# Three edits of a planner's ranks and margins in the FFN of a perceiver layer

## The chip, the core and the metric

The kernel runs on one NeuronCore of a Trainium2 chip. The metric is the device time of one launch in microseconds. A profile of one execution is shown beside it; its times count from the first instruction of the span.

## What is computed

The reference is one layer with three residual blocks on 16 x 64 rows of 1024 (1024 rows in all, in float32):

```python
x = x + cross_attention(layernorm(x), ctx, ctx, mask)      # 32 query heads, 8 kv heads, 1601 keys
s = silu(layernorm(x) @ w_gate.T)                          # 2752 columns
s[the K = 1376 smallest |s| of each row] = 0               # top_k(-abs(s), k)
x = x + (s * (layernorm(x) @ w_up.T)) @ w_down.T
logits = layernorm(x) @ router_w.T + router_b              # 8 experts, 2 chosen per row
x = x + sum over chosen e of gate[e] * (layernorm(x) @ A[e].T) @ Bm[e].T * 0.5
```

The change lies in the second and third blocks, which the kernel runs together as its FFN phase.

## The kernel before

The 1024 rows are eight tiles of 128 rows. The first half of the span (to about 840 us) is attention. The FFN phase takes the tiles in four pairs: pair n is tiles 2n and 2n + 1. For every pair there are three products with large weights, named in the code g (gate), u (up) and d (down): g0 to g3, u0 to u3, d0 to d3. Each is a Strassen-like scheme: instead of eight quarter products it has seven, each with a sum of quarters of the rows and a sum of quarters of the weights. The sums of the weights are made during attention and lie in DRAM (`ts`).

The stages of one pair are:

- Normalising (`normed`, from `measured`): ACT computes a mean and a sum of squares, POOL makes the inverse root and a shift, ACT scales the row tile. The rows are first loaded again from DRAM (`xs`) into the tile `s`.
- `quad_turned` transposes four blocks on PE (`pt_f` in the trace) and copies them out of PSUM on ACT. `gate` adds the four sums of quarters in `hS`, on DVE for the first pair and on POOL for the others.
- `widen` runs the units of g and u: one unit is one of seven products on one of four chunks of columns, eight matmul rows of the trace (`pg_g`, `pg_u`), about 2.3 us. DVE and ACT sum the products; ACT applies silu to g, POOL multiplies u in.
- `drop_small` is the choice of the zeroed elements. It is a search over 31 bits for a threshold per row; each step is a compare on DVE (`junk`) for the first tile of the pair, a sign on ACT (`sign`) for the second, and a short settling on DVE (`cand`). Scans follow on DVE (`rank`), and POOL multiplies the zeros into `s`.
- `turned` transposes `s` (`ptd` on PE, copies on ACT), and `down` runs d: seven products (in the order 1, 5, 7, 6, 2, 3, 4), each in four parts (`pd`). The row sums that it needs are made on POOL in parts (`S`, and sums in place in `s`). DVE and POOL add the products to the residual `xd`.
- `experts` runs once per tile, after its two sums of d: it transposes x (`pt_m`, copied to `xT`), multiplies by the router and the A matrices (`pl`), chooses, transposes (`ph`) and multiplies by Bm (`py`); DVE writes the result, and SP stores it.

The order of instructions on PE, DVE, ACT and POOL is not written by hand. Every piece above is a task with an engine, a cost in microseconds, the tasks it depends on, a rank, and the buffers it takes and frees. `Plan.run` walks through planned time. Whenever an engine is free, it starts the task of lowest rank (and of earliest creation among equals) whose dependencies have ended and whose buffers are free. A task with a margin also waits until each dependency has ended for that long. The order in which tasks are started is the order in which they are emitted, and each of these four engines then runs its own list strictly in that order.

The ranks that matter here are these. Copies and sums are at 0. The transposes of the experts are at 0 or -1. The last signs and the scans of a choice are at 2, the compares and signs of its search at 3. Normalising for pairs 1 to 3, and transposing and summing for their gates, are at 5. The large products have ranks 10, 20, ... by their place in one list, and the transposes and sums on POOL of a d follow the rank of that d (one lower, or the same):

```python
order = ["g0", "u0", "g1", "g2", "d0", "u1", "g3", "d1", "u2", "d2", "u3", "d3"]
rank = {name: 10 + 10 * j for j, name in enumerate(order)}
```

Three groups of buffers bind the stages. Five PSUM banks (`pg`) serve all large products. Two PSUM banks (`px`) serve all transposes and the experts. One hold named `opening` is taken by the first unit of every chunk of g and u and by the first part of every d, and is given back by product 7 of the chunk or by the first part of product 6 of the d. Two tiles of sums (`hS`) exist, so gate 3 can be transposed only when u1 has read the tile of pair 1. Tiles 6 and 7 also reuse the `s` tiles of tiles 0 and 1, so their rows are loaded after the results of those tiles are stored, and their normalising has a margin of 30 us after that start.

Weights come through a ring of six tiles, loaded by DMAs on SP: one of 688 KB per unit of g or u, and one of 768 or 512 KB per part of a d.

Of the kernel before, what the change touches and what calls it, by code (L numbers as in the profile page):

```python
# [21 lines left out]
B, S, D = 16, 64, 1024  # L22
T, C = 1601, 256
HD = 32
NT = B * S // P
# [29 lines left out]
def tile_perceiver_layer(  # L55
# [306 lines left out]
    def finish_tile(i, h, home=ps_t, tag="pt"):  # L362


        if h == 0:
            att[i] = xnp.tile([P, 2, 4, 4, HD], F32, tag="xn", name=f"att{i}")
        rows = att[i][:, h]
        pt = home.tile([P, 4, P], F32, tag=tag, name=f"pto{i}_{h}")
        for r in range(4):
            pe.transpose(  # L370
                pt[:, r, :], oT[i][:, h, r].rearrange("p b s -> p (b s)"), ident
            )

        def add():
            pool.tensor_tensor(
                rows, rows, rs_tok[i][:, h].unsqueeze(3).to_broadcast([P, 4, 4, HD]),
                ALU.mult,
            )
            xv = x[i].rearrange("p (h g r d) -> p h r g d", h=2, g=4, r=4)
            pool.tensor_tensor(xv[:, h], xv[:, h], rows, ALU.add)  # L380

        return (rows, pt.rearrange("p r (g d) -> p r g d", g=4)), add
# [34 lines left out]
    first, first_xn = (xnp, otp), {}  # L417
    for n in range(ng):
        i, m = n // 8 + 1, n % 8
# [10 lines left out]
        for d in range(2):  # L430
            add = None
# [6 lines left out]
            if n > 8 and 3 <= 2 * m + d <= 4:  # L438
                copy, add = finish_tile(i - 2, 1 - d)
# [89 lines left out]
    def px_tile(shape, name):  # L529
        return ps_x.tile(shape, F32, tag="px", name=name)  # L530

    plan = Plan({"pg": 5, "px": 2, "u": 2, "v": 3, "hS": 2, "opening": 1, "S1": 1})
    add = plan.add
    s, hS, held_h, hs, a, marked = {}, {}, {}, {}, {}, {0: [], 1: []}
# [16 lines left out]
        nc.sync.dma_start(w, home[q, :, c0:c1])  # L551
        return w

    def quad_turned(src, dst, rank, name, after, takes=None):

        box, px = {}, plan.hold("px")

        def turn():
            pt = px_tile([P, 4, P], f"pt_{name}")
            for j in range(4):  # L560
                pe.transpose(pt[:, j, :], src()[:, j * P : (j + 1) * P], ident)
            box["pt"] = pt

        def copy():
            act.copy(dst(), box["pt"])

        t = add("PE", 0.55, turn, after, rank, takes=(px, takes))
        return add("ACT", 0.55, copy, [t], 0, frees=px)

    def measured(rows, junk, rank, name, after, margin=0.0, on_dve=0):  # L570
# [44 lines left out]
    def normed(rows, xn, rank, name, after, margin=0.0):  # L615

        box, t = measured(rows, xn, rank, name, after, margin)

        def shift():
            box["shift"] = small.tile([P, 1], F32, tag="shift", name=f"shift_{name}")  # L620
            pool.tensor_tensor(box["shift"], box["minus"], box["rstd"], ALU.mult)

        def scale():
            act.activation(xn(), rows(), AF.Identity, bias=box["shift"], scale=box["rstd"])

        t = add("POOL", 0.3, shift, [t], rank)
        return add("ACT", 1.1, scale, [t], rank)
# [89 lines left out]
    def gate(pair, n, rank, after):  # L717
        i1, i2 = pair
        engine, name, cost = (dve, "DVE", 0.62) if n == 0 else (pool, "POOL", 1.25)
        turned, ahead = [], 5 if n else rank  # L720
        held_h[n] = plan.hold("hS")

        def quarters(q):
            if n not in hS:
                hS[n] = hsp.tile([P, 7, NH // 2, P], F32, tag="hS", name=f"hS{n}")
            return hS[n][:, q]

        for i in pair:

            def start(i=i):  # L730
                s[i] = sp[i % 6 > 1].tile([P, NIB * P], F32, tag="s", name=f"s{i}")
                pool.memset(s[i][:, I:], 0.0)
                if i not in first_xn:
                    nc.sync.dma_start(s[i][:, D : 2 * D], xs[i])

            t = add("POOL", 0.1, start, after(i), rank)
            if i not in first_xn:
                t = normed(
                    lambda i=i: s[i][:, D : 2 * D], lambda i=i: s[i][:, :D], ahead,
                    f"f{i}", [t], 30.0,  # L740
                )
            for half, q in enumerate((A11, A12) if i == i1 else (A21, A22)):
                turned.append(
                    quad_turned(
                        lambda i=i, half=half: first_xn.get(i, s[i])[
                            :, half * HC : (half + 1) * HC
                        ],
                        lambda q=q: quarters(q), ahead, f"f{i}_{half}", [t] + turned[:1],
                        None if turned else held_h[n],
                    )  # L750
                )

        def summed(dst, q0, q1, op):
            return lambda: engine.tensor_tensor(
                *(hS[n][:, q].rearrange("p k t -> p (k t)") for q in (dst, q0, q1)), op
            )

        hs[n] = turned
        t11, t12, t21, t22 = turned
        t1 = add(name, cost, summed(S1, A21, A22, ALU.add), [t21, t22], ahead)  # L760
        t2 = add(name, cost, summed(S2, S1, A11, ALU.subtract), [t1, t11], ahead)
        t3 = add(name, cost, summed(S3, A11, A21, ALU.subtract), [t1, t11], ahead)
        t4 = add(name, cost, summed(S4, A12, S2, ALU.subtract), [t2, t12], ahead)
        ready = {1: t11, 2: t12, 3: t4, 4: t22, 5: t1, 6: t2, 7: t3}
        return widen(0, n, pair, rank, f"g{n}", lambda p: [ready[p]] + (p == 6) * [t1, t3], None)
# [317 lines left out]
    def experts(i, after):  # L1083
# [15 lines left out]
        def h3T():  # L1099
            if "xT" not in box:  # L1100
                xT = sump.tile([P, NB * P], F32, tag="S1", name=f"xT{i}")
                box["xT"] = xT[:, :D].rearrange("p (c t) -> p c t", c=NH)
            return box["xT"]
# [71 lines left out]
        def copy():  # L1175
# [4 lines left out]
        norm, t = measured(  # L1180
            lambda: x[i], lambda: s[i][:, :D], 1, f"m{i}", after,
            on_dve=(1 + i % 2) * (i >= NT - 2),
        )
        copies, pl, ph = [], plan.hold(kind), plan.hold(kind)
        xT, first = plan.hold("S1"), i % 2
        for g in (first, 1 - first):
            copies.append(
                quad_turned(
                    lambda g=g: x[i][:, g * HC : (g + 1) * HC],
                    lambda g=g: h3T()[:, 4 * g : 4 * g + 4, :], urgent, f"m{i}_{g}",  # L1190
                    after[g : g + 1] + copies + ([logits_of[i - 1]] if i % 2 else []),
                    xT if g == first else None,
                )
            )
        tl = add("PE", 2.1, logits, copies, urgent, takes=pl, frees=xT)
# [12 lines left out]
        t = add("DVE", 1.2, choose, [tb], 1)  # L1208
        t = add("DVE", 0.5, weigh, [te, t], 1)
        add("DVE", 0.6, normaliser, [t], 1)  # L1210
        t = add("PE", 0.2, turn, [t], 0, takes=ph)
        t = add("ACT", 0.3, copy, [t], 0, frees=ph)
# [19 lines left out]
        return done  # L1232

    pairs = [(i, i + 1) for i in range(0, NT, 2)]
    order = ["g0", "u0", "g1", "g2", "d0", "u1", "g3", "d1", "u2", "d2", "u3", "d3"]
    rank = {name: 10 + 10 * j for j, name in enumerate(order)}
    gated = [gate(pairs[0], 0, rank["g0"], lambda i: [])]

    t = add("PE", 2.9, lambda: groups[-1].values(0, NTC), [], rank["g0"] - 5)
    t = add("ACT", 0.3, lambda: groups[-1].keep(), [t], 0)  # L1240
# [8 lines left out]

    over = add("PE", 1.1, end, [t] + hs[0], rank["g0"] - 5)  # L1250
    gated += [gate(pairs[n], n, rank[f"g{n}"], lambda i: [over]) for n in (1, 2)]

    box_ra, held_ra = {}, plan.hold("px")
# [10 lines left out]
    t = add("DVE", 1.3, sum_blocks, [over], rank["g1"], margin=30.0)  # L1264
    t = add("PE", 0.25, sum_rows, [t], rank["g0"], takes=held_ra)
# [4 lines left out]
    for n, pair in enumerate(pairs):  # L1270
        kept, t = drop_small(
            pair, n, gated[n], chosen,
            lambda t: widen(1, n, pair, rank[f"u{n}"], f"u{n}", lambda p: t, t),
        )
# [12 lines left out]
class Plan:  # L1287
# [20 lines left out]
    def add(self, engine, cost, emit, deps, rank, takes=None, frees=None, margin=0.0):  # L1308
        holds, frees = (
            [hold for hold in (h if isinstance(h, tuple) else (h,)) if hold]  # L1310
            for h in (takes, frees)
        )
        task = self.Task(engine, cost, emit, deps, rank, holds, margin)
        for hold in frees:
            hold.freed_by = task
        self.tasks.append(task)
        return task
# [98 lines left out]
```

## Time and profile before

| | |
|---|---|
| median of 3 runs | 1720.96 us (1720.15 to 1721.5) |
| the profiled execution | 1721.3 us |
| its span, first to last instruction | 1719.5 us |
| mean granted TensorE clock | 0.995 |
| busy PE, DVE, ACT, POOL | 1694.0, 1413.0, 1259.6, 557.2 us |
| attention, to about | 840 us |
| pd rows of d0, about | 1127 to 1196 us |
| pg_u rows of u1, about | 1112 to 1258 us |
| pd rows of d1, about | 1265 to 1413 us |
| pg_g rows of g3, about | 1308 to 1378 us |
| pd rows of d2 | 1501 to 1571 us |
| pd rows of d3 | 1633 to 1706 us |

PE is the TensorE's matmuls and PEld its weight loads, DVE is VectorE, ACT ScalarE, POOL GpSimd and SP the engine that issues most DMAs. A row of the timeline has its start, its duration in microseconds (of one instruction, or of several merged), and the operation with the tiles it writes and reads; a number in brackets at its end is the time its engine stood idle before it and the instruction that ended the wait. PEclk is the share of its full clock that TensorE was granted.

### The profile page before, as it was taken

The numbers are of one execution on the slowest core, as the hardware profiler recorded it, in microseconds if no ns is written. First come the engines' busy times: TensorE is split into PE (matmuls) and PEld (weight loads), VectorE is DVE, ScalarE is ACT, GpSimd is POOL, SyncE is SP. The second block draws the span as 40 slices with busy tenths as digits, with TensorE's granted clock in tenths as the row PEclk, the third lists the DMA queues.
The fourth block names the chain that finished last, engine by engine and source line by source line (L and its number), as shares of the span: only waits on it lengthen the run. The fifth ranks groups of instructions, "written<-read, shape, count | busy, mean of one in ns | idle before, by whom it ended". The sixth has DMA issues, their size and how long they took to land. (4 is left out here: it accounts for less than half of the span.)

```text
span 1719.5 us, 38732 instructions
## 1 busy us (share of the span) xinstructions
PE 1694.0 (99%) x15102; PEld 1152.2 (67%) x15102; DVE 1413.0 (82%) x3655; ACT 1259.6 (73%) x1780; POOL 557.2 (32%) x584
## 2 busy tenths in 40 slices
PE   8999999999999999999999999999989999999999
PEld 6777777777777777777766666655645646645644
DVE  7888888888888888888627999999999989999703
ACT  5999999999999999999544676577657782778010
POOL 2045454454444454110120211222282013331631
PEclk9999999999999999999999999999999999999999
DMA  8246456555556646121499999988969978888984
GB/s 248 74 122 207 148 194 210 188 166 195 170 185 206 204 159 208 57 75 58 182 349 324 308 292 304 302 267 291 324 202 292 309 251 301 283 294 270 316 265 143
DMA packets 132327, 384.56 MB, mean 224 GB/s; under 512 B 9489, under 2 KB 61233, under 8 KB 132145
## 3 DMA queue, kind: packets, MB, share of 16 engines
q1 hardware_dynamic: 113280, 312.83, 55.5%
q0 software_dynamic: 18432, 68.16, 12.1%
q8 instruction: 120, 1.97, 0.5%
q10 hardware_dynamic: 432, 1.09, 0.2%
q14 instruction: 63, 0.51, 0.1%
HBM read 339.58 MB, written 42.47 MB: 222 GB/s over the span
## 5 line engine op out<-in xcount | busy, mean ns | idle before, releaser
L93 DVE CUSTOM_DVE_ANT_0 sc<-ps,mask 128x512 f32<-128x512 f32 (+2 forms) x1024 | 526.4, 571 | 104.8 <-PE ps L93 104.4
L93 ACT ACTIVATE sign<-a,cand 128x2752 int8<-128x2752 f32 x136 | 351.9, 2587 | 110.9 <-DVE cand L93 110.5
L93 ACT ACTIVATE sc<-sc,nm 128x1601 f32<-128x1601 f32 x256 | 420.2, 1667 | 11.5 <-DVE nm L93 11.5
L93 PEld LDWEIGHTS pt<-ident,sc 128*128 128x128 f32 (+1 forms) x3328 | 361.9, 141 | 77.3 <-issue 72.8
L93 PE MATMUL pt<-ident,sc 128*128 128x128 f32 (+1 forms) x3328 | 391.1, 274 | 1.0 <-ACT sc L93 0.9
L93 DVE TENSOR_SCALAR_CACHE_REDUCE junk<-a,cand 128x2752 uint8<-128x2752 f32 x124 | 381.7, 3078 | 4.0
L93 ACT COPY pT<-pt 128x512 f32<-128x512 f32 x636 | 323.9, 609 | 46.5 <-PE pt L93 46.2
L93 PE MATMUL pg_g<-w_g,hS 128*128 128x344 f32 x896 | 261.2, 453 | 2.6 <-DMA w_g<-ts 1.8
L93 PE MATMUL pg_u<-w_u,hS 128*128 128x344 f32 x896 | 263.4, 452 | 0.0
L93 POOL TENSOR_TENSOR tw<-tw 128x344 f32<-128x344 f32 (+1 forms) x192 | 175.9, 927 | 265.5 <-DMA tw<-in_wg_dram 87.3
L93 PE MATMUL ps<-kT,qt 32*128 32x512 f32 (+2 forms) x2048 | 248.1, 550 | 4.6 <-DMA kT<-in_ctx_t_dram 3.4
L93 PE MATMUL pd<-w_d,s 128*128 128x512 f32 x528 | 235.2, 599 | 0.0
L93 PEld LDWEIGHTS pg_g<-w_g,hS 128*128 128x128 f32 x896 | 169.5, 190 | 91.0 <-issue 3.3
L93 PEld LDWEIGHTS pg_u<-w_u,hS 128*128 128x128 f32 x896 | 168.8, 190 | 87.4 <-issue 3.4
L93 PE MATMUL po<-pT,v 128*32 128x128 f32 x6656 | 208.2, 274 | 0.4 <-ACT oT L93 0.4
L93 PEld LDWEIGHTS po<-pT,v 128*32 128x32 f32 x6656 | 174.1, 110 | 48.6 <-issue 45.7
L93 PEld LDWEIGHTS pd<-w_d,s 128*128 128x128 f32 x528 | 99.9, 193 | 115.7 <-issue 114.6
L93 DVE COPY pT<-pt 65x128 f32<-65x128 f32 (+1 forms) x388 | 141.0, 418 | 22.9 <-PE pt L93 16.0
L93 PEld LDWEIGHTS ps<-kT,qt 32*128 32x128 f32 x2048 | 83.3, 184 | 53.9 <-DVE mx L93 36.7
L93 ACT ACTIVATE s<-s 128x344 f32<-128x344 f32 (+1 forms) x70 | 36.6, 535 | 74.8 <-DVE s L93 74.7
L93 POOL TENSOR_TENSOR s<-s,rank 128x688 f32<-128x688 f32 x32 | 62.4, 1965 | 77.3 <-DVE rank L93 76.7
L93 DVE DVE_READ_ACCUMULATOR2_ANT mx<- 128x1 f32 x1024 | 84.0, 82 | 0.0
(322 smaller groups left out, 1216.6 us busy)
## 6 DMA issues: line engine op xcount, KB each, us to landing
w_g<-ts SPq DMA_DIRECT2D x64, 688.0 KB
w_u<-ts SPq DMA_DIRECT2D x64, 688.0 KB
w_d<-ts SPq DMA_DIRECT2D x48, 768.0 KB
w_g<-in_wg_dram SPq DMA_DIRECT2D x48, 688.0 KB
w_u<-in_wu_dram SPq DMA_DIRECT2D x48, 688.0 KB
w_d<-in_wd_dram SPq DMA_DIRECT2D x36, 768.0 KB
kT<-in_ctx_t_dram SPq DMA_DIRECT2D x31, 800.5 KB
v<-in_ctx_v_dram SPq DMA_DIRECT2D x32, 768.0 KB
```

The lines of the kernel that those rows point to most:

```text
L93: return tc.keep_in_program_order(getattr(self.engine, op)(*args, **kwargs))
```

## The change

There are three edits. Normalising the rows of pairs 1 to 3 gets rank 2 instead of 5, which is lower than the 3 of a choice's compares and signs; the transposes and sums of these gates stay at 5. The experts' transposes of tiles 0 to 5 get a margin of 2.0 us behind all they depend on. And d1 comes ahead of g3 in the list, so that d1 has rank 70 (its transposes 69) and g3 rank 80.

```diff
-    def quad_turned(src, dst, rank, name, after, takes=None):
+    def quad_turned(src, dst, rank, name, after, takes=None, margin=0.0):
...
-        t = add("PE", 0.55, turn, after, rank, takes=(px, takes))
+        t = add("PE", 0.55, turn, after, rank, takes=(px, takes), margin=margin)
...
                 t = normed(
-                    lambda i=i: s[i][:, D : 2 * D], lambda i=i: s[i][:, :D], ahead,
+                    lambda i=i: s[i][:, D : 2 * D], lambda i=i: s[i][:, :D],
+                    min(ahead, 2),
                     f"f{i}", [t], 30.0,
                 )
...
                     after[g : g + 1] + copies + ([logits_of[i - 1]] if i % 2 else []),
-                    xT if g == first else None,
+                    xT if g == first else None, 2.0 * (i < NT - 2),
...
-    order = ["g0", "u0", "g1", "g2", "d0", "u1", "g3", "d1", "u2", "d2", "u3", "d3"]
+    order = ["g0", "u0", "g1", "g2", "d0", "u1", "d1", "g3", "u2", "d2", "u3", "d3"]
```

## The prediction

> **What bounds the kernel now.** I read the page's first two parts, then PE's waits, PE in order of time where those waits lie, and last the engines that end them.
>
> ```profile
> span 1719.5 us, 38732 instructions
> PE 1694.0 (99%) x15102; PEld 1152.2 (67%) x15102; DVE 1413.0 (82%) x3655; ACT 1259.6 (73%) x1780; POOL 557.2 (32%) x584
> PEclk9999999999999999999999999999999999999999
> ```
>
> TensorE is busy 99% of the span, and the change takes no matmul away and adds none. It can only take away or add PE's waits, and the stretches of half clock behind them. In the FFN (840 us to the end) PE's waits add to 14 us; these are the largest and those the change touches:
>
> ```profile
> PE ptd L93 <- ACT s L93: 3.8, 4, 2.1
> PE pt_f L93 <- ACT s L93: 2.6, 1, 2.6
> PE pt_m L93 <- DVE xd L93: 2.2, 1, 2.2
> PE pl L93 <- DVE s L93: 0.8, 2, 0.7
> PE pd L93 <- POOL S L93: 0.6, 1, 0.6
> ```
>
> In order of time they stand in two places, A (1258 to 1283) and B (1390):
>
> ```profile
> 1258.35 0.60 PE L93 MATMUL ptd<-ident,s 128*128 128x128 f32 x4
> 1261.56 0.66 PE L93 MATMUL pt_f<-ident,s 128*128 128x128 f32 x4 [2.61 <-ACT s L93]
> 1264.34 1.11 PE L93 MATMUL ptd<-ident,s 128*128 128x128 f32 x4 [2.13 <-ACT s L93]
> 1281.42 0.93 PE L93 MATMUL ptd<-ident,s 128*128 128x128 f32 x6 [1.01 <-ACT s L93]
> 1282.99 2.84 PE L93 MATMUL pd<-w_d,S 128*128 128x512 f32 x6 [0.64 <-POOL S L93]
> 1291.36 1.04 PE L93 MATMUL pt_f<-ident,s 128*128 128x128 f32 x8
> ...
> 1392.02 0.95 PE L93 MATMUL pt_m<-ident,xd 128*128 128x128 f32 x4 [2.23 <-DVE xd L93]
> ```
>
> The number in brackets is PE's idle time before the row. At A, u1 has ended and d1 begins, and nothing else may run; at B, d1's last sums reach the experts late. The clock over these stretches (columns: busy time of PE, PEld, DVE, ACT, POOL, then PEclk):
>
> ```profile
> 862.00:866.00 4.00, 2.16 (x9) 1.15 (x8) 0.52 (x1) 0.49 (x1) 0.00 (x0) 1.00 1.03 428
> 1262.00:1266.00 4.00, 1.87 (x7) 1.25 (x6) 4.00 (x3) 3.25 (x7) 3.96 (x2) 0.57 0.03 14
> 1266.00:1270.00 4.00, 4.00 (x8) 1.61 (x7) 4.00 (x3) 0.08 (x1) 4.00 (x3) 0.58 0.00 0
> 1388.00:1392.00 4.00, 1.79 (x5) 0.48 (x3) 3.93 (x6) 2.68 (x2) 0.03 (x1) 1.00 0.99 350
> 1392.00:1396.00 4.00, 3.98 (x9) 2.17 (x10) 3.70 (x7) 3.24 (x4) 0.00 (x0) 0.57 0.38 147
> ```
>
> Both idle stretches are followed by half clock; a wait of 1.84 us near 864 was not.
>
> **The sum's base.** The profiled execution took 1721.3 us (span 1719.5 and 1.8 around it), 0.3 above the median of 1720.96. What a measurement of this kernel can tell from no change is about 0.2%, or 3.4 us.
>
> **Margin of 2 us on the experts' transposes (tiles 0 to 5).** It adds no instruction. Where the plan would put a pt_m at the planned end of the sum it needs, it now puts another unit of 2.3 to 2.6 us in front. At B, the pd rows end at 1389.79 and DVE's sum xd comes at 1391.28 to 1391.97, behind a choice's compare of 3.08 us that started at 1388.28. One unit of d1 (6 pd, 2.57 us) in front covers 2.23 us. With the wait goes its half clock: the 28 pd behind it took 13.62 us where the 28 ahead took 12.18, and the pt_m 0.95 where others take 0.60, so 1.44 + 0.35 = 1.8. Gain at B: **4.0**. For tiles 0 and 1, tile 1's second pt_m (1202.66) and tile 0's second py move behind one pg_u unit (2.31 us) more, and tile 0's second result behind one more compare on DVE. That removes the wait of 0.17 at 1209.78: **0.2**. The late result holds its output DMA on SP's queue and, behind that, tile 6's reload into s (1213.11) some 3.5 us. The normalisation of tile 6 waits at least 30 us after that start and has POOL in front of it anyway (below), so nothing is late. Waits next in line, 0.56 (py on ACT's hwT) and 0.66 at 1578.96, I leave as they are.
>
> **Normalising ahead of the signs (rank 5 to 2 for tiles 2 to 7).** No instruction is added. Tiles 2 to 5 are normalised at 878 to 902, before the first sign (920.85): nothing to overtake, worth nothing; if the POOL steps of tile 5 slip ahead of gate 1's sums, these end 1 us later than 898.7, and are first used at 915.7. Tile 6's mean (1243.92) comes after the last sign of choice 1 and its scale (1260.26) waits for POOL:
>
> ```profile
> 1255.42 3.63 POOL L93 TENSOR_TENSOR s<-s,v_u_(2, 0)_16296 128x344 f32<-128x344 f32 x1
> 1259.14 0.19 POOL L93 TENSOR_SCALAR ve_f<-sq_f 128x1 f32<-128x1 f32 x1
> 1276.48 0.19 POOL L93 TENSOR_TENSOR shift_f<-minus_f,rstd_f 128x1 f32<-128x1 f32 x1
> 1287.88 1.28 ACT L93 ACTIVATE s<-s,shift_f,rstd_f 128x1024 f32<-128x1024 f32 x1
> 1293.15 5.09 POOL L93 TENSOR_TENSOR hS<-hS 128x512 f32<-128x512 f32 x4
> ```
>
> POOL's products stand ahead at rank 0 by either rank. So A's 2.61 and 2.13 stay: **0**. Only tile 7's scale moves. It could go at 1276.7 (shift) and went at 1287.88, behind three signs of choice 2. With rank 2 it follows ACT's copies that end at 1281.8, ahead of the sign at 1281.73. That sign then ends 2.2 us later (scale 1.14 and two copies in front), which DVE's next settle waits out; but the 1.14 at 1287.88 goes, so choice 2 ends as before.
>
> What it triggers matters more. The two pt_f (0.88 together) come at about 1285.7 instead of 1291.36, their copies at 1286.6 to 1287.6, and then gate 3's four hS sums on POOL are ready. They have rank 5, d1's own S sums rank 70 or 80. POOL began d1's sums at 1281.94, about 1 us each; some seven are done at 1288.9, then four hS sums take 5.09, to 1294.0, and only then comes the sum that product 5's fourth part needs (it was emitted at 1288.89; its last transposed block is later now by two pt_f on PE and one sign on ACT). It takes 0.73, to 1294.7. PE meanwhile: product 5's first part to 1285.67, pt_f to 1286.55, second part to 1289.1, a last ptd pair 0.26, third part to 1291.9. It waits 1291.9 to 1294.7, 2.8 us. Nothing covers this: g3 and u2 both need the single "opening", which d1 gives back at product 6. The fourth part started at 1292.24 before: **+2.5**.
>
> What the clock makes of 2.8 us idle: the rows say 2.23 idle was enough for a stretch of half clock worth 1.8, and 1.84 was not. [...] I take **+1.1**, bounds 0 and 1.8.
>
> **d1 ahead of g3.** On PE, g3's 28 units stood between d1's parts, from 1308.6 to 1377.6 (32 pg_g, 10 pd, 192 pg_g); now d1 runs on, g3 follows. The work moved is 28 units of 8 pg_g at 2.31 us, 64.7 us, with one weight DMA of 688 KB each on SP, past d1's remaining w_d DMAs of 768 and 512 KB, POOL's four sums at 1380 to 1388 and three products of xd. Order alone costs PE nothing: d0 and d2 ran unbroken from 1127 to 1197 and from 1501 to 1571 with PE busy 69.95 of 70 us in both. Cover for d1's waits: g3 after product 6, as u1 is for d0. SP: in those stretches DMA was at 0.85, against 0.89 with g3 inside, so weights keep up; without that, each late one costs what w_g did at 863 (1.8). g3 ends at about 1418 instead of 1377.6; its silus are needed by choice 3, which begins at 1443.6. The experts of tiles 2 and 3 move from 1392 to 1442 to about 1330 to 1360, among choice 2's signs and g3's silus. That adds at most two ACT table loads (1.28 each, as at 1413.74) and some 8 us of DVE work to the search, and takes the latter from the scans behind it. Choice 2 can slip by up to 11 us (8.6 DVE, 2.6 loads) with no relief, 0 to 3 with it. Its own turns come only at 1484, but choice 3 follows it: its last keep ends at 1617.9 and the first ptd of d3 is at 1631.3, with a POOL product of 1.5 between. About 11 us of cover, so **0**; past it, microsecond for microsecond.
>
> **Sum.** 1721.3 - 4.0 - 0.2 + 2.5 + 1.1 = **1720.7**, 0.3 under the median: no difference that could be told.
>
> **The rivals.**
>
> *Gain without the price.* POOL finishes d1's sums ahead of the hS sums, or the fourth part's sum slips in front. Then B's 4.2 is left whole, and the two pt_f (0.88) fall into A's 1.65 us of small waits at 1281: 1721.3 - 4.2 - 0.9 = 1716.2. For it: PE ran 2.6 us units while POOL needs 1 us a sum, so POOL has room. Against: rank 5 before 70, and the last block's copy is behind a sign.
>
> *Slower: gate 3's sums stand ahead of all of d1's on POOL.* If the scale is placed in the gap ahead of the copies (1276.7), pt_f and hS sums come before POOL's first S sum. PE's 0.64 at 1282.99 grows by 5.1 and joins the 1.01: an idle stretch like A's first, with two windows of half clock (there 6 pd took 4.79 instead of 2.74 and a ptd group 0.5 more: 2.6). 1721.3 - 4.2 + 5.1 + 2.6 = 1724.8. It decides from the point where the new idle and its clock cost more than 4.2 + 3.4. For it: ACT was idle 1.62 us before 1280.29. Against: two copies of rank 0 were ready at 1277.6, and transposes need one of two px banks.
>
> *It does not do what it says:* 80 of d1's 154 pd rows ran ahead of g3's first unit anyway, and the moved scale may find ACT taken as before: 1721.
>
> **How the numbers follow.** Forecast 0.38 (own range 1718.5 to 1723.5; within 0.2% of the median 0.28, 0.05 either side), gain without price 0.32 (faster 0.29, 0.03 within), slower 0.26 (slower 0.23, 0.03 within), nothing done 0.04. Together: faster 0.34, same 0.38, slower 0.28. The range reaches from just under the second case to just over the third: 1715.5 to 1726.
>
> **What would show it.** Right: no pt_m wait near 1390 or later; PE's 2.61 on pt_f and 2.13 on ptd still at 1258 to 1264, with two windows of half clock; tile 7's scale at about 1282 ahead of a sign; hS sums on POOL at about 1289, in the middle of S sums; a wait "pd <- POOL S" of 2 to 3 us near 1292; g3 in one piece, at about 1345 to 1418. Wrong: that pd wait under 1 us (first rival) or over 4 (second); A's waits gone, which would mean that f6's path moved too; or ptd waiting for POOL at 1631, if choice 3 became late.

## The result, and the profile after

The changed kernel takes 1723.83 us (median of 22 runs, 1721.22 to 1727.21), beside 1721.37 for the kernel before in the same set (22 runs, 1719.37 to 1724.47). The ratio is 1.0013, 95% interval 1.0007 to 1.0019. The profiled execution took 1723.33 us, its span is 1721.5. So the change costs about 2.3 us (1.2 to 3.3), where the forecast had 0.3 us of gain. The loss is small, but it is outside the interval of no change, and it is a sum of larger terms of both signs.

The page of the changed kernel, with the lines that answer to those of before:

```profile
span 1721.5 us, 38744 instructions
PE 1692.4 (98%) x15102; PEld 1151.1 (67%) x15102; DVE 1411.4 (82%) x3655; ACT 1262.7 (73%) x1782; POOL 561.8 (33%) x584
PEclk9999999999999999999999999999999999999999
```

The matmuls are the same; ACT has two instructions more, both table loads (seven for five, 1.28 us each). PE's waits from 840 us on (total, times, longest):

```profile
PE pd L93 <- POOL S L93: 3.2, 2, 2.5
PE ph L93 <- DVE adj L93: 3.0, 2, 2.0
PE ptd L93 <- ACT s L93: 2.9, 4, 1.4
PE pt_f L93 <- ACT s L93: 2.3, 1, 2.3
PE pl L93 <- ACT xT L93: 0.9, 1, 0.9
```

The 2.2 us of pt_m on DVE's xd are gone. In their place stand 2.5 us more of pd on POOL's S, and ph and pl, which wait for the experts' small steps and were nearly absent before. PE in order of time at place A and behind it, where the last bracket of 2.51 is the new wait:

```profile
1261.44 1.12 PE L93 MATMUL pt_f<-ident,s 128*128 128x128 f32 x4 [2.33 <-ACT s L93]
...
1275.00 1.06 PE L93 MATMUL ptd<-ident,s 128*128 128x128 f32 x8 [1.38 <-ACT s L93]
1278.65 1.06 PE L93 MATMUL ptd<-ident,s 128*128 128x128 f32 x8 [0.86 <-ACT s L93]
1280.14 0.93 PE L93 MATMUL ptd<-ident,s 128*128 128x128 f32 x6 [0.43 <-ACT s L93]
1281.71 2.84 PE L93 MATMUL pd<-w_d,S 128*128 128x512 f32 x6 [0.64 <-POOL S L93]
1284.39 1.04 PE L93 MATMUL pt_f<-ident,s 128*128 128x128 f32 x8
...
1293.32 1.98 PE L93 MATMUL pd<-w_d,S 128*128 128x512 f32 x4 [2.51 <-POOL S L93]
```

The engines that make it, ACT with tile 7's scale and POOL with the fourth gate's four sums in front of d1's:

```profile
1280.45 1.26 ACT L93 ACTIVATE s<-s,shift_f,rstd_f 128x1024 f32<-128x1024 f32 x1
```

```profile
1287.49 5.09 POOL L93 TENSOR_TENSOR hS<-hS 128x512 f32<-128x512 f32 x4
1292.54 0.72 POOL L93 TENSOR_TENSOR S<-s 128x256 f32<-128x256 f32 x1
```

And PE where the time is lost, at the experts of tiles 4 and 5 between d2 and the end of u3:

```profile
1567.03 1.19 PE L93 MATMUL pl<-ra_sb,xT 128*128 128x136 f32 x8 [0.88 <-ACT xT L93]
1574.27 0.33 PE L93 MATMUL ph<-ident,adj 128*128 128x128 f32 x1 [0.98 <-DVE adj L93]
1576.75 0.60 PE L93 MATMUL pt_m<-ident,xd 128*128 128x128 f32 x4
1584.02 2.12 PE L93 MATMUL pl<-ra_sb,xT 128*128 128x136 f32 x16 [0.33 <-DVE s L93]
1595.06 0.33 PE L93 MATMUL ph<-ident,adj 128*128 128x128 f32 x1 [1.97 <-DVE adj L93]
1595.22 4.16 PE L93 MATMUL pg_u<-w_u,hS 128*128 128x344 f32 x8
```

The kernel before had one wait in this stretch, of 0.66 us. Its rows that answer to the last four are:

```profile
1573.64 0.63 PE L93 MATMUL pt_m<-ident,xd 128*128 128x128 f32 x4
1578.96 2.12 PE L93 MATMUL pl<-ra_sb,xT 128*128 128x136 f32 x16 [0.66 <-DVE s L93]
1592.49 0.27 PE L93 MATMUL ph<-ident,adj 128*128 128x128 f32 x1
1592.60 2.48 PE L93 MATMUL pg_u<-w_u,hS 128*128 128x344 f32 x8
```

The waits of the changed kernel add to 4.16 us. Its eight pg_u rows took 4.16 us too, where the same eight took 2.48 before: half clock again (PEclk 0.50 from 1595.85 to 1599.27).

To see where the time went, I cut the FFN at rows that every kernel has, and took the time between them: u1 (from the first ptd of d0 to the first ptd of d1), A (on to d1's first pd that reads S), d1 to d2 (on to d2's first pd) and d2 to d3 (on to d3's first ptd).

| profiled execution | u1 | A | d1 to d2 | d2 to d3 |
|---|---|---|---|---|
| before | 146.56 | 24.64 | 218.04 | 130.30 |
| after | 145.57 | 23.20 | 215.93 | 135.69 |
| difference | -0.99 | -1.44 | -2.11 | +5.39 |

Ahead of these the changed execution lost 0.85 in attention and 0.30 in the first gates, and behind them nothing; together +2.0, the difference of the spans. The point where the first gate begins lay between 845.1 and 847.6 us over all the kernels, with the same attention, so that 0.85 is no effect of the change. The four stages alone leave a loss of 0.85 us, less than the 2.3 of the medians; stretches of half clock differ from trace to trace (see the section on the hardware), and one trace of each kernel settles no more than this.

So 4.5 us were gained in three stages, and 5.4 lost in the fourth, where the prediction had no term at all.

### The profile page after: what moved, and what is told of

It is laid out like the page before. It is cut to its first block, busy times and chain, and to the rows that moved or that the text cites. A ratio compares the mean times of both kernels' runs of the same rounds, so it can differ in the third digit from the quotient of the medians.

```text
span 1721.5 us, 38744 instructions
## 1 busy us (share of the span) xinstructions
PE 1692.4 (98%) x15102; PEld 1151.1 (67%) x15102; DVE 1411.4 (82%) x3655; ACT 1262.7 (73%) x1782; POOL 561.8 (33%) x584
## 3 DMA queue, kind: packets, MB, share of 16 engines
q8 instruction: 120, 1.97, 0.5%
```

## The experiments

Twelve more kernels ran beside the kernel before. M is the margin, O the order, R the rank; M03 is the margin on tiles 0 to 3 alone. Stages are in us, from one profiled execution each.

| kernel | ratio to before, interval | u1 | A | d1 to d2 | d2 to d3 |
|---|---|---|---|---|---|
| M | 0.9992 (0.9983 to 1.0001) | 145.58 | 23.18 | 215.84 | 132.12 |
| O | 0.9986 (0.9977 to 0.9995) | 146.54 | 24.69 | 214.41 | 131.30 |
| R | 1.0013 (1.0004 to 1.0022) | 146.55 | 24.95 | 221.10 | 130.30 |
| O and M | 0.9964 (0.9951 to 0.9976) | 145.58 | 23.16 | 213.05 | 131.89 |
| O and R | 0.9993 (0.9984 to 1.0002) | 146.52 | 23.51 | 217.60 | 131.15 |
| R and M | 1.0001 (0.9992 to 1.0009) | 145.58 | 25.31 | 217.18 | 132.14 |
| O, R, M (the change) | 1.0013 (1.0007 to 1.0019) | 145.57 | 23.20 | 215.93 | 135.69 |
| O and M03 | 0.9965 (0.9952 to 0.9977) | 145.56 | 25.27 | 213.03 | 131.31 |
| O, R, M03 | 0.9985 (0.9976 to 0.9994) | 145.59 | 23.17 | 215.92 | 131.23 |

A stretch of half clock is in some of these cells and not in others. In "d1 to d2" it stands in before (at 1392), R (at 1396), O (at 1284) and O-and-R (at 1293), in "d2 to d3" in the change (at 1596), and it costs about 1.4 to 1.7 us there (at 1392 in before 28 pd rows took 13.62 for 12.18, at 1596 in the change eight pg_u rows 4.16 for 2.48). R has another at 1283, most of which a wait behind it took up. In A, R-and-M and O-and-M03 have two in a row (at 1272 to 1279), which cost 2.1. With that in mind the columns read plainly. The margin sets the first column. The third has three levels in the main: 218 for before, 213 for the order without the rank (O had half clock on top), 216 for the order with it (O-and-R had half clock on top); M alone is at 216 too.

**The change with the margin on tiles 0 to 3 alone.**

```diff
-                    xT if g == first else None, 2.0 * (i < NT - 2),
+                    xT if g == first else None, 2.0 * (i < NT - 4),
```

> The changed kernel, with the margin for tiles 0 to 3 only. In the changed kernel PE lost 5.4 us between d2 and the end of u3: 0.88 (pl on xT), 0.98 and 1.97 (ph on adj), 0.33, and about 1.7 of half clock. Theory M (the margin on tiles 4 and 5 moves tile 5's choice behind a second scan on DVE): the 1.97 at 1595 and its half clock go, perhaps the 0.88 too; 0.98 stays if it is the table load. Then 3.7 to 4.6 us faster than the changed kernel, so about 1 to 2 us faster than before. Theory C (DVE and ACT run tiles 4 and 5 in line with the search of choice 3, whose pace did not change; PE came 3.4 us earlier and must wait for them whatever the margin): the waits move to other rows of the same tiles and add up to about 3.4 us again; the time stays 2 us above before.

Measured: 1718.72 us (11 runs, 1715.94 to 1722.59), against 1721.57 of before. Everything up to d2 is as in the changed kernel (215.92 and 215.93), since the planner has made the same list so far. Behind d2 the stage is 131.23 instead of 135.69. That is theory M: the margin on tiles 4 and 5, in this plan, costs 4.5 us, and the changed kernel without it is faster than before.

**The change without any margin.**

```diff
-                    xT if g == first else None, 2.0 * (i < NT - 2),
+                    xT if g == first else None, 0.0,
```

> The changed kernel with no margin at all: ranks and order only. Forecast of the prediction's step for the margin: the wait at the first pt_m of tile 2 comes back only if PE is ahead of its plan there; after the new wait of 2.5 us PE is behind, so I expect no pt_m wait of 2 us and the same time up to d1. Behind d2: by theory M as without the margin on tiles 4 and 5, about 1 to 2 us faster than before; by theory C 2 us slower than before, as the changed kernel.

Measured: 1720.74 us (11 runs). No wait of pt_m of 2 us is left even without the margin, so something else in the change removes it as well; the kernel with the order alone (below) shows that it is the order. Behind d2 the stage is 131.15, as theory M had it. In stage u1 the waits of 0.17 and 0.56 are back (146.52), so these are most of what the margin on tiles 0 and 1 is worth. Behind the POOL wait stands half clock here:

```profile
1292.22 2.86 PE L93 MATMUL pd<-w_d,S 128*128 128x512 f32 x4 [2.51 <-POOL S L93]
```

The same four rows took 1.98 in the changed kernel, behind the same wait of 2.51.

**The margin alone, and order with margin.** Each takes the other edits back:

```diff
-                    min(ahead, 2),
+                    ahead,
...
-    order = ["g0", "u0", "g1", "g2", "d0", "u1", "d1", "g3", "u2", "d2", "u3", "d3"]
+    order = ["g0", "u0", "g1", "g2", "d0", "u1", "g3", "d1", "u2", "d2", "u3", "d3"]
```

> Before, with the margin of 2 us on tiles 0 to 5 as the only edit. By the prediction: the pt_m wait of 2.23 us at 1392 goes and with it its half clock, 4.0 us. By theory M tiles 4 and 5 then lose 3 to 5 us near 1590: about the same as before in all (-1 to +1). By theory C too, since PE would come 4 us earlier to the same search: the waits would be of rows of tiles 4 and 5 (0.98 for the table load is not among them here).

> The changed kernel with the old rank 5 for normalising: order and margin only. By the prediction: the wait of d1 on POOL's S near 1293 (2.5 us) goes, since the hS sums come behind all S sums again. PE then reaches d2 some 2.5 us earlier than in the changed kernel. Theory M: 2.5 us faster than the changed kernel, the loss on tiles 4 and 5 as there. Theory C: no gain, the waits on tiles 4 and 5 grow by about 2.5 us.

Order with margin has the first of these two edits alone. Measured: the margin alone 1719.67 us (11 runs), order with margin 1715.91 us (5 runs), both beside 1721.57. The margin alone also removes the wait at 1392 and its half clock, which were priced at 4.0 us. But "d1 to d2" falls by only 2.2, since the small steps of the experts of tiles 2 and 3 now keep PE waiting:

```profile
1409.46 1.19 PE L93 MATMUL pl<-ra_sb,xT 128*128 128x136 f32 x8 [0.46 <-ACT xT L93]
1421.14 0.30 PE L93 MATMUL ph<-ident,adj 128*128 128x128 f32 x1 [0.35 <-DVE den L93]
1432.82 0.33 PE L93 MATMUL ph<-ident,adj 128*128 128x128 f32 x1 [0.86 <-DVE adj L93]
```

Behind d2 it pays again, at tile 5, as the changed kernel does:

```profile
1593.09 0.33 PE L93 MATMUL ph<-ident,adj 128*128 128x128 f32 x1 [2.50 <-DVE adj L93]
```

Order with margin is faster than before by 0.36% (0.24 to 0.49%), and than the changed kernel by some 8 us. The rank, which alone tells these two apart, costs 2.9 us between d1 and d2 (213.05 to 215.93) and 3.8 between d2 and d3. Neither theory had the second: M expected the loss at tiles 4 and 5 to stay as it was without the rank, C expected it to grow. In the kernel without it POOL takes the sums in the other order:

```profile
1288.54 0.73 POOL L93 TENSOR_TENSOR S<-s 128x256 f32<-128x256 f32 x1
1289.34 0.73 POOL L93 TENSOR_TENSOR s<-s,s 128x256 f32<-128x256 f32 x1
1290.03 2.65 POOL L93 TENSOR_TENSOR s<-S,s 128x384 f32<-128x384 f32 x3
1292.79 5.09 POOL L93 TENSOR_TENSOR hS<-hS 128x512 f32<-128x512 f32 x4
```

The first line is the sum that PE waits for in the changed kernel; here it is done 4 us earlier, and the four hS sums harm nobody behind it.

**The order alone.** The edit is the order line of the change and nothing else.

> The before kernel with the new order alone (d1 ahead of the fourth gate), no margin, old rank. My prediction put the order alone at 0 and the wait at 1392 down to the missing margin: that theory gives the time of before, about 1721, with a pt_m wait of 2 us still there. The other theory, after the run without margin (which had no pt_m wait of 2 us left), is that the order alone takes the wait at 1392 and its half clock away, because no fourth-gate unit and no compare lie between d1's last sums and the experts as they did: 1717 to 1718 (4.0 less). The waits of 2.6 and 2.1 on pt_f and ptd stay in both, the POOL wait of 2.5 is in neither.

Measured: 1718.28 us (11 runs) against 1720.90; the second theory. The wait of 2.23 at 1392 is gone; the next wait of a pt_m is one of 0.44 at tile 4 (1559). "d1 to d2" falls by 3.6 although a stretch of half clock fell at 1284 in this execution; order with margin, which has none there, shows 5.0.

**Order, and margin on tiles 0 to 3, with the old rank.**

> New order, old rank, margin on the transposes of tiles 0 to 3 alone. Theory 1: the margin on tiles 4 and 5 costs about 4.5 us by itself wherever it stands; then this is 4 to 5 us under the run with order and margin on tiles 0 to 5 (1715.9), about 1711.5. Theory 2: with the old rank that margin costs nothing, since tile 5's choice of experts was not held behind a whole second scan there (135.7 us from d2 to the end of u3 in the changed kernel, 131.9 with the old rank); the loss needs the plan that the new rank makes: then 1715 to 1716.5, and d2 to the end of u3 within 1 us of 131.9.

Measured: 1714.65 us (5 runs, 1713.97 to 1717.82), ratio 0.9965; the second theory. The margin on tiles 4 and 5 costs only 0.6 in the stage here (131.31 to 131.89). Compare its price in the four pairs of kernels that differ by it: 1.8 (before to M), 1.8 (R to R-and-M; in these two the margin on tiles 0 to 3 comes with it, but that acts ahead of this stage), 0.6 (here) and 4.5 (the change). It is a gain in none of the four. In the kernel before nothing waited at d2's end that it could remove; with the new order and M03 tile 4's pt_m waits 0.66 here and 0.98 in the kernel with the rank, and the margin does remove that, but pays more for it behind. How much depends on how the whole list falls.

**One more exponential, so that the table is there ahead of tile 4's choice.** On order with margin:

```diff
+            def preload():
+                y = small.tile([P, 1], F32, tag="sq", name="sq_table")
+                act.activation(y, neg_half, AF.Exp)
+
+            add("ACT", 0.3, preload, [d for i in pairs[3] for d in gated[3][i]], 0)
```

> Order and margin with the old rank (1715.9), and one more ACT instruction: an exponential of one column behind the fourth gate's last silu, so that the exponential table is in place long before tile 4's choice. If the wait of 0.97 us of tile 4's ph on DVE's adj (1571) comes from the table load of 1.28 us directly in front of p, that wait goes and the time is 1714.5 to 1715.3, with the load at about 1417 beside u2 and no ACT table load near 1569. If the wait is DVE's own order (the choice's compare and sum in front of adj), the load moves and the wait and the time stay, 1715.9.

Measured: 1716.13 us (6 runs); the same as without it. The load moved as it should:

```profile
1415.65 1.28 ACT L93 ACT_TABLE_LOAD   x1
1416.95 0.20 ACT L93 ACTIVATE sq_table<-neg_half 128x1 f32<-128x1 f32 x1
```

But tile 4's steps kept PE as long:

```profile
1568.04 0.33 PE L93 MATMUL ph<-ident,adj 128*128 128x128 f32 x1 [0.78 <-DVE adj L93]
1571.68 1.98 PE L93 MATMUL py<-bm_sb,hwT 128*128 128x512 f32 x4 [0.56 <-ACT hwT L93]
1592.13 1.98 PE L93 MATMUL py<-bm_sb,hwT 128*128 128x512 f32 x4 [0.31 <-ACT hwT L93]
```

So the load of 1.28 us just ahead of p looks like the cause of ph's wait in the trace, and is not: without it DVE's own chain is nearly as late (0.78 for 0.97).

**The changed kernel's list, with the four hS sums five POOL instructions later.** The planned order is kept; only these four emissions are held back.

```diff
-                    task.emit()
+                    if engine == "POOL" and n_h3 < 4 and task.late:
+                        n_h3 += 1
+                        behind.append(task.emit)
+                    else:
+                        task.emit()
+                        if engine == "POOL" and n_h3 == 4:
+                            past += 1
+                            while past == 5 and behind:
+                                behind.pop(0)()
```

> The changed kernel (order, margin, new rank) with its plan untouched, except that POOL issues the fourth gate's four hS sums five instructions later, behind d1's last S sums of products 5 and 7. It measures the price of the hS sums by itself. Theory P: the wait of 2.5 us of pd on POOL's S near 1292 goes, and it is worth itself (no half clock stood behind it in the trace): d2's first pd comes 2.5 us earlier and the time is 1721.3, 2.5 under the changed kernel. Theory C: what the second down gains is given back at the experts of tiles 4 and 5, because the choice of the fourth pair runs at its own pace and is reached too early: the wait goes, but d2 to the end of u3 grows by 1 to 2.5 us and the time is 1722 to 1723.8.

Measured: 1721.42 us (11 runs, ratio 1.0001, 0.9992 to 1.0010). The wait of 2.51 is gone, and PE runs 2.8 us earlier at product 7 (from d1's first pd on S). But by 1347 only 0.7 of it is left. Its own waits, in the stretch of the experts of tiles 2 and 3:

```profile
1321.19 5.42 PE L93 MATMUL pd<-w_d,s 128*128 128x512 f32 x12 [0.29 <-POOL s L93]
...
1340.74 1.19 PE L93 MATMUL pl<-ra_sb,xT 128*128 128x136 f32 x8 [0.32 <-ACT xT L93]
...
1346.71 0.30 PE L93 MATMUL ph<-ident,adj 128*128 128x128 f32 x1 [0.74 <-DVE den L93]
```

DVE shows why. Tile 2's weighted adj in the changed kernel, and then in this one:

```profile
1346.25 0.29 DVE L93 TENSOR_TENSOR adj<-adj,wt 128x128 f32<-128x128 f32 x1
```

```profile
1346.27 0.29 DVE L93 TENSOR_TENSOR adj<-adj,wt 128x128 f32<-128x128 f32 x1
```

DVE reaches it at the same time in both, since compares and signs of the choice set its pace, and not PE. That is theory C, with its place some 220 us earlier than I had it: the gain is given back at the experts of tiles 2 and 3. Between d2 and d3 nothing changed (135.66). The median fell by more than the trace accounts for (the ratios differ by 0.0012; one is uncertain by 0.0006, the other by 0.0009), so the size of the gain stays open between 0.7 and some 4 us.

**The changed kernel's list, with the choice of tile 5's experts ahead of a scan.** Again only an emission is moved: the fourth choice's second scan on DVE, behind the normaliser of tile 5.

```diff
+                t[0].late = (n, j, h) == (3, 0, 1)
...
-        add("DVE", 0.6, normaliser, [t], 1)
+        add("DVE", 0.6, normaliser, [t], 1).last = i == 5
...
-                    task.emit()
+                    if task.late:
+                        behind.append(task.emit)
+                    else:
+                        task.emit()
+                        while task.last and behind:
+                            behind.pop(0)()
```

> The changed kernel with its plan untouched, except that DVE gets the fourth choice's second scan (0.93 and 3.02 us) behind tile 5's choice of experts instead of in front of it. Theory: the 4.5 us lost between d2 and the end of u3 are in the main this: tile 5's logits are there at 1586.1, but its first DVE step waits behind the scan until 1590.9, so PE waits 1.97 at 1595 and runs its next 8 pg_u at half clock (4.16 for 2.48). Then both go, d2 to the end of u3 falls from 135.7 to about 132, and the time is 1720.1, 3.7 under the changed kernel; the waits of 0.88 and 0.98 for tile 4 stay. Rival: the choice then ends about 3 us later, POOL's last products of the fourth pair are late, and d3's first ptd wait for what was gained: stage 134 to 136, time 1722 to 1724.

Measured: 1720.44 us (11 runs, ratio 0.9991, 0.9982 to 1.0000), 3.4 less than the changed kernel by the medians and 3.8 by the ratios. The changed kernel has the scan in front of tile 5's first step on DVE:

```profile
1587.56 3.02 DVE L93 TENSOR_TENSOR_SCAN rank<-junk 128x1376 int16<-128x1376 uint8 x1
1590.50 0.49 DVE L93 TENSOR_TENSOR v_u_(6, 1)_18192<-pg_u,u_u 128x344 f32<-128x344 f32 x1
1590.91 0.34 DVE L93 SCALAR_TENSOR_TENSOR adj<-ra_sums,minus_m,pl 128x136 f32<-128x136 f32 x1
```

With the scan behind it, PE in this kernel has neither the wait nor the half clock:

```profile
1593.83 0.33 PE L93 MATMUL ph<-ident,adj 128*128 128x128 f32 x1
1594.00 2.48 PE L93 MATMUL pg_u<-w_u,hS 128*128 128x344 f32 x8
```

The stage falls from 135.69 to 132.60, and the rival's late choice did not come about (d3's first wait is 0.24 in both). So of the 5.4 us lost, 3.1 are this one scan; the rest is in the main tile 4's 0.88 and 0.98, which this kernel still has.

**Order, margin on tiles 0 to 3, and the exponential.** The second diff above on top of the kernel with order and M03.

> Order, old rank, margin on tiles 0 to 3, and the exponential behind the fourth gate's last silu: the version that the runs so far point to. In the run without the exponential (1714.65) tile 4's ph waited 1.35 us on adj, with a table load of 1.28 us at 1563.3 directly ahead of it. If that load makes the wait: 1713.3 to 1714, and d2 to the end of u3 about 130.2. The same edit on the kernel with margin on tiles 0 to 5 took 0.2 us off that wait and gave two waits of 0.56 and 0.31 on py in return, with the time the same; if that is how it goes here too: 1714.6.

Measured: 1715.53 us (5 runs, ratio 0.9967): no faster than without the exponential. The wait of 1.35 on tile 4's adj became 0.92. Order with margin, with M or M03, with or without the exponential, stays the fastest version; the four cannot be told apart.

**The rank alone, and rank with margin.**

> The before kernel with the new rank of the normalising alone: old order, no margin. If the price of the fourth gate's hS sums ahead of d1's S sums is the same in the old order (2.4 us there by the run that issued them later), a POOL wait of 2.5 us stands near 1292 and the wait of 2.2 near 1392 stays with its half clock: 1723.8. Rival: with the old order the fourth gate's first unit is in front of d1's last product and can take that time: 1721.4, the time of before.

> Old order with the new rank and the margin on tiles 0 to 5. The margin alone gave 1719.7 here. With the price of the hS sums 1722.1. If the loss of 4.5 us at the experts of tiles 4 and 5 comes from new rank and margin together whatever the order: 1726 to 1727, with d2 to the end of u3 above 135. If it belongs to the one plan that all three parts make: 1722, with that stage at 130 to 132.5.

Measured: 1723.33 us for the rank alone (ratio 1.0013), 1721.29 with the margin (ratio 1.0001), beside 1721.21. The first is as the price says, but it is made up otherwise: the POOL wait is 1.21 and not 2.5, because six pd rows at half clock ahead of it (4.54 us for 2.84) had made PE 1.7 late. POOL's sum comes when it comes: the fourth part starts 12.0 us behind A's end here and 11.6 in R-and-M, so that of 1.7 us of half clock 0.4 was paid. The second gives 132.14 between d2 and d3: the loss of 5.4 belongs to the one list that all three edits make, the theory's "whatever the order" is refuted.

## Why the prediction was wrong

**The step that failed is "Waits next in line, 0.56 (py on ACT's hwT) and 0.66 at 1578.96, I leave as they are".** The margin holds for tiles 0 to 5; I priced it where it would help, at B and at tiles 0 and 1, and gave tiles 4 and 5 nothing because nothing waited there. But a margin delays a transposition at every tile, and behind tiles 4 and 5 stands a chain of small steps over ACT and DVE (xT, pl, adj, p, ph, py) that shares DVE with the fourth choice's scans. In the changed kernel tile 5's second pt_m starts 79.1 us behind d2's first pd, 72.6 in the kernel before, though the sum that it needs ends only 0.5 later. That puts pl behind the first scan and adj behind the second. In the kernel before, this chain lay across the scans too, but its ph stood five pg_u units behind its pl in PE's list, not three, and did not wait.

The price is 5.4 us in the profiled execution, of which 1.7 is half clock. It is the whole of the miss and more: without it (margin on tiles 0 to 3) the change gains 0.15% (0.06 to 0.24). That the second scan makes 3.1 of it is shown by moving that scan. The rest is read from the waits at tile 4, and no experiment took it out by itself.

Point by point, by the prediction's own terms:

- *B, 4.0 of gain.* The wait and its half clock went, but the margin alone did not earn the 4.0: it took 2.2 off the stage, and 1.7 came back as waits at the experts of tiles 2 and 3. This is the failed step again, at other tiles. The order alone removes the same wait, so that it is not worth nothing, as I had it, but about as much as the whole of B (3.6 in that stage with a stretch of half clock in it, 5.0 with the margin beside it and no stretch). Two edits take the same wait, and it is luck that I counted it once.
- *Tiles 0 and 1, 0.2.* It was 1.0: the 0.56 that I left standing went too.
- *"A's 2.61 and 2.13 stay".* Half right. The sum of A's waits on ACT (2.61, 2.13, 1.01) is now 2.33, 1.38, 0.86 and 0.43, which is 0.75 less, and the half clock lasts 3.41 us (1261.35 to 1264.76) where it lasted 6.83 (1262.54 to 1269.37); the stage is 1.4 shorter, and 23.2 with every list that has the margin and no half clock behind 1272. The 2.13 went with the margin (it is gone with M and stays with R): tile 7's rows are loaded again at 1236.90 instead of 1228.25, and its two first passes on ACT no longer stand between tile 6's scale and the copies that PE waits for. Most of the 1.4 is the clock, since the kernel without margin keeps the waits (2.60 and 2.12), has one stretch of half clock of some 3.4 us there, and takes 23.51.
- *The POOL wait, 2.5.* Right, when the 1.3 us by which A ended earlier are taken off: scale at 1280.45 (forecast 1281.8), hS sums at 1287.5 (1288.9), a wait of 2.51 (2.8), and the fourth part 2.4 later behind A's end than before (2.5).
- *Its half clock, 1.1.* No run shows this term. In the changed kernel no half clock came behind the wait of 2.51; of the five kernels with a wait of 2.5 here, one had it, the kernel without margin (2.86 us for the four pd rows that took 1.98 in the changed kernel). There 2.45 us of one window were idle, in the other four kernels at most 1.8 (the next section has the windows).
- *What stands behind the POOL wait.* I took the wait to be the whole price of the rank. With the wait taken out, 0.7 of the stage came back and about 2.2 stayed. So "choice 2 ends as before" was wrong; counted from A's end, its last rank row on DVE ends 2.7 us later than with the old rank. In the changed kernel DVE's settle waits 2.71 us at 1285 for the sign that the scale had pushed back; the kernel with the old rank has 0.82 there.
- *"At most two table loads", off the path.* There were two more in all, one of them directly ahead of tile 4's p. Moving it away changed no time, so the price of 0 was right.
- *The gate behind d1 in one piece.* Right: its rows run from 1345 to 1416. (Ahead of its first unit the kernel before has 78 pd rows, not 80.)

With the measured sizes the sum is -1.0 - 1.4 - 2.1 + 5.4 = +0.9 in the four stages, where the forecast had -0.2, 0, -0.4 and 0. The rest of the spans' 2.0 is the 1.15 that the profiled execution lost ahead of them.

Of the rivals, the one that ended slower had the right sign and the wrong mechanism. The hS sums did not come ahead of all of d1's sums, and A's end was not lengthened.

## What the runs showed of the hardware

The fourteen traces have 24 stretches of half clock between 840 us and the last rows. 19 of them last 3.4 us, as in the changed kernel from 1261.35 to 1264.76 and from 1595.85 to 1599.27, and five twice that, as in the kernel before from 1262.54 to 1269.37. The two of the changed kernel begin 334.50 us apart, which is 98 times 3.413, and those of the kernel before (1262.54 and 1392.25) 129.71, which is 38 times 3.413; in the other traces with more than one stretch the starts lie whole multiples of it apart too, to within 0.1 us. So I cut every trace into windows of this length, counted from its stretches, and took PE's idle time in each window at full clock. With more than 2.1 us idle (19 windows) half clock always followed, with 1.6 to 2.1 in 5 of 13, with less never.

So in these traces half clock goes not with the length of a wait, but with how much of it falls into one window. The changed kernel has a wait of 2.51 us cut in halves by a window's edge at 1292.07 (1.27 and 1.25 us idle on its two sides), and one of 1.97 that lies in one window (columns: busy time of PE, PEld, DVE, ACT, POOL, then PEclk):

```profile
1288.66:1292.07 3.41, 2.14 (x5) 0.60 (x4) 3.29 (x3) 2.97 (x4) 3.33 (x4) 1.00 0.69 181
1292.07:1295.49 3.42, 2.17 (x5) 1.06 (x6) 3.24 (x5) 2.68 (x2) 3.34 (x5) 1.00 0.50 205
1592.44:1595.85 3.41, 1.44 (x7) 0.69 (x6) 3.17 (x10) 0.27 (x1) 0.91 (x1) 1.00 0.96 323
1595.85:1599.27 3.42, 3.42 (x8) 1.98 (x7) 2.67 (x5) 0.00 (x0) 0.91 (x1) 0.50 0.26 103
```

In the kernel without margin, the same wait of 2.51 lies almost whole in one window:

```profile
1289.77:1293.18 3.41, 0.96 (x2) 0.49 (x3) 3.23 (x5) 2.51 (x3) 3.33 (x5) 1.00 0.74 238
1293.18:1296.60 3.42, 3.42 (x6) 1.35 (x5) 2.95 (x6) 1.16 (x2) 2.40 (x3) 0.50 0.23 39
```

The first gate's wait for weights at 863 shows the same: 2.4 to 3.1 us in six traces, with a stretch behind it in five (in the sixth, R-and-M, an edge leaves no more than 1.55 in one window), and 1.6 to 2.1 in the other eight, with none. At 1.4 to 1.7 us a stretch, two stretches alone make some 3 us between one trace and another (my estimate from the rows above), which is as much as the whole change.

Nor did every stretch cost its 1.4 to 1.7 us. In A the changed kernel has one at 1261.35 and takes 23.20; the same list with the hS sums later has none there and takes 23.17. There PE only waited longer for the next copy, 2.96 instead of 1.38:

```profile
1275.06 1.06 PE L93 MATMUL ptd<-ident,s 128*128 128x128 f32 x8 [2.96 <-ACT s L93]
```

## What to carry to other kernels

In a list made by a planner, price an edit at every place where its condition holds, not only where it helps, and above all where many small steps of two engines share a queue with long instructions: here the margin put tile 5's adj behind a scan of 3.02 us. Take a change of three edits apart before judging it: two of the three here gain 0.36% together, and the third gives it all back. And before removing a wait, look at what the engine that ends the next wait is doing: if it runs at its own pace, as DVE did here (tile 2's adj at 1346.25 and 1346.27), the time comes back a few rows later under another name. Of the five waits of 2.5 us on POOL's S here, one had half clock behind it, by where a window's edge fell in that execution; so the half clock of one trace is not the price of an edit.
